# Two transformer layers on one core: operands split by ScalarE's rounding instead of a mask, a chunk's splitting moved behind the keys, first rows transposed tile by tile, epsilon put into the statistics

## Chip, cores, metric

The kernel runs on one core of a Trainium2 chip. The metric is the device time of one execution in microseconds. Engines are named as the profile does: PE (TensorE; PEld is its weight load), DVE (VectorE), ACT (ScalarE), POOL (GpSimd), SP (SyncE, whose queue issues most DMAs).

## What is computed

The reference, cut to what matters. `x` is [2, 512, 512] in float32; B=2, S=512, HID=512, INTER=1376.

```python
x = _layernorm(x + _L0_attn_ref(x, ...))   # retrieval from a memory M: q = elu(x@Wq.T+bq)+1 in
                                           # 8 heads, (q@M)/(q@z+1e-6), repeated, @ Wo.T
x = _layernorm(x + _L0_ffn_ref(x, ...))    # ternary weights, silu(gate)*up, truncated to int8 twice
x = _layernorm(x + _L1_attn_ref(x, ...))   # one head of 128: softmax(q@k.T/sqrt(128)) @ v, @ Wo + bo
x = _layernorm(x + _L1_ffn_ref(x, ...))    # silu(x@w_gate.T) * (x@w_up.T), @ w_down.T, all float32
```

with `_layernorm(x) = (x - mean) / sqrt(var + 1e-5)` over the last axis.

## The kernel before, in words

**Tiles.** A batch row block is 512 tokens: four tiles `x_b_t` of 128 tokens by 512 columns. Products want the columns on partitions, so the tiles are transposed on PE, 128x128 at a time, into a PSUM bank `pt`, and copied to SBUF. PSUM is one pool of eight banks of 128x512 (`psum`), handed out in turn: a new tile waits until the one eight before it is read.

**Order.** On PE, DVE, ACT and SP the order of instructions on each engine is set when the kernel is built, by the framework's scheduler; `tc.issue_after(i)` is a tie that puts what follows it behind instruction `i` in that order. POOL's order is the order of the program.[...]

**Layer 0, attention.** `load_x(0)` (L85) sends four tiles, on SP's and ACT's queues in turn; then come `wq_0`, `bq`, `z` and the other heads' weights on SP's queue (L307 to L311). `rise` (L108) is a set of products of `ones` with itself that no result uses. `transposed(xs[0], "a00", cuts=2)` (L444) transposes two tiles, then the other two, each time with four copies by ACT and DVE (L129). `queries` (L341) makes a head's queries, head 0 in two halves of 256 tokens. The heads' outputs, normalised, go on to layer 0's FFN (products L556 and L611), whose ternary values are checked and coded.

**Layer 1, attention.** For each batch: transposes, queries and keys (`pqk`, L842; evicted by ACT with bias, L847), values (`pv`, L855; DVE adds bv, L859). POOL adds `bo` to the rows (L906). Then scores (`psc`, L870), DVE's row maxima (L876), ACT's exponentials (L892), transposes of the probabilities (`pt_p`, L124), products with the values (`pot`, L927, copied to `ot`, L931), and `output` (L942: `po`, L944). `attended` (L947) divides by the sum and adds the row; `norm_a1` normalises: statistics on DVE, `root` (L160) and two `off` steps on POOL (L938, L939), and the scaling on ACT (L940).

**Layer 1, FFN.** Full float32 accuracy from three products in fp32r[...]: each operand is split into h, its upper part, l, the rest, and d, a combination of both. `cut` (L748) makes the upper part m on DVE by masking the lower bits away. `weight_parts` (L757) takes m, 4096·w by ACT (`big`, two buffers), h as ACT's copy of m, l = big − 4096·m and d = l − m on DVE. `row_parts` (L767) does so for rows. INTER is cut into eleven chunks, ten of 128 and one of 96; `turn = [6..10, 0..5]` is their order. The splitting of the first three chunks (`split_up(0)`, `(1)`, `(2)`; L790) lies within layer 1's attention: two while batch 1's transposes are copied, the third behind the last row maximum and ahead of the reciprocals. Later ones, and those of the down weights (`split_down`, L1096) and of the products' results (`split_tile`, L1103), are called in the loop over steps (L1163). `split_rows` (L970) transposes a batch's normalised rows and splits them; for batch 1 and for k > 0 ACT copies the bank to SBUF first (L982).

`up1` (L1071) is a step: gate and up products of one chunk and one batch (24 products, L1039), summed by ACT and DVE (`sum_up`), Silu on ACT and the product of both on DVE. The first step of a batch goes through its products block by block as rows become ready. `down1` (L1119) makes the down products (L1130) for one tile of 128 tokens, adds them, normalises and sends the rows; the very last tile is done in two halves of 256 columns (`cuts` = 2). Its `else` branch (L1145) is the end of the kernel: variance plus epsilon on DVE (L1147), power −1/2 on POOL (L1148), mean subtracted and the first half scaled on DVE (L1149, L1150), the other half on ACT (L1151), and two sends (L1155).

Of the kernel before, what the change touches and what calls it, by code (L numbers as in the profile page):

```python
# [19 lines left out]
P = 128  # L20
# [16 lines left out]
def kernel(  # L37
# [47 lines left out]
    def load_x(b):  # L85
        for t in range(NT):
            x = xp.tile([P, HID], F32, tag="x", name=f"x_{b}_{t}")
            eng = nc.scalar if b == 0 and t % 2 else nc.sync
            eng.dma_start(x, x_in[b, ts(t, P), :])
            xs[b].append(x)  # L90

    load_x(0)
    bq = const.tile([D, NH], F32, tag="bq", name="bq")
    z = const.tile([D, NH], F32, tag="z", name="z")

    make_identity(nc, ident)
# [8 lines left out]
    nc.vector.memset(ones, 1.0)  # L105
# [9 lines left out]
    def transposed(rows, name, cuts=0, in_turn=False):  # L115


        xt = xtp.tile([P, NK, S], F32, tag="xt", name=f"xt_{name}")
        pts = {}

        def turn(k, t, i=0):
            if (k, i) not in pts:
                pts[k, i] = psum(f"pt_{name}_{k}_{i}")
            return nc.tensor.transpose(  # L124
                pts[k, i][:, ts(t, P)], rows[t][:, ts(k, P)], ident
            )

        def copy(k, at, i=0):
            move = nc.vector.tensor_copy if k == 1 or k % 2 > in_turn else nc.scalar.copy  # L129
            copies.append(move(xt[:, k, at], pts[k, i][:, at]))  # L130

        if cuts:
            for i in range(cuts):
                for t in range(i * NT // cuts, (i + 1) * NT // cuts):
                    for k in range(NK):
                        turn(k, t, i)
                for k in range(NK):
                    copy(k, ts(i, S // cuts), i)
        else:
            done = None  # L140
            for k in range(NK):
                with ExitStack() as tied:
                    if in_turn and k:
                        tied.enter_context(tc.issue_after(done.ins))
                    for t in range(NT):
                        done = turn(k, t)
                copy(k, slice(0, S))
        return xt
# [152 lines left out]
    with tc.tile_pool(name="a0w", bufs=1) as a0w, tc.tile_pool(name="a0", bufs=2) as a0:  # L301
        wq = []
        for h in range(NH):
# [5 lines left out]
            if h == 0:  # L309
                nc.sync.dma_start(bq, bq_in)  # L310
                nc.sync.dma_start(z, z_in)  # L311
# [29 lines left out]
        def queries(b, xt, h, cuts=1):  # L341

            pq = psum(f"pq_{b}_{h}")
            for i in range(cuts):
                at = ts(i, S // cuts)
                for k in range(NK):
                    nc.tensor.matmul(  # L347
                        pq[:, at], wq[h][:, k, :], xt[:, k, at],
                        start=(k == 0), stop=(k == NK - 1),
                    )  # L350
# [7 lines left out]
            qs[b].append(q)  # L358

# [84 lines left out]
        xt = transposed(xs[0], "a00", cuts=2)  # L444
        for h in range(NH):
            queries(0, xt, h, 1 if h else 2)
# [296 lines left out]

    BIG = 4096.0
    MAIN, CROSS = 1.0 + 1.0 / BIG, 1.0 / BIG
    cutp = ctx.enter_context(tc.tile_pool(name="cutp", bufs=2))

    def cut(src, w, name):  # L748

        m = cutp.tile([P, 512], F32, tag="cut", name=f"m_{name}")  # L750
        p = src.shape[0]
        nc.vector.tensor_single_scalar(
            m[:p, :w].bitcast(I32), src.bitcast(I32), TOP12, ALU.bitwise_and
        )
        return m[:p, :w]

    def weight_parts(w, parts, name):  # L757

        h, l, d = parts
        m = cut(w, 512, name)  # L760
        big = cutp.tile([P, 512], F32, tag="big", name=f"big_{name}")
        nc.scalar.activation(big, w, AF.Copy, scale=BIG)
        nc.scalar.copy(h, m)
        nc.vector.scalar_tensor_tensor(l, m, -BIG, big, ALU.mult, ALU.add)
        return nc.vector.tensor_sub(d, l.bitcast(F32), m)  # L765

    def row_parts(src, m, parts):  # L767

        h, l, d = parts
        moved = nc.scalar.copy(h, m)  # L770
        nc.vector.tensor_sub(l, src, m)
        return moved, nc.vector.scalar_tensor_tensor(
            d, l.bitcast(F32), -BIG, m, ALU.mult, ALU.add
        )
# [15 lines left out]
    def split_up(j, room):  # L790
# [3 lines left out]
        for a in range(2):  # L794
# [5 lines left out]
            if n == P or a == 0:  # L800
                done = weight_parts(w, up_parts[j, a], f"gu{j}_{a}")
                continue

            u, m, w = (
                v.rearrange("p (k i) -> p k i", k=NK)
                for v in (up_parts[j, a][0], cut(w, NK * P // 2, f"gu{j}_{a}"), w)
            )
            nc.scalar.copy(u[:, :, : P // 2], m)
            done = nc.vector.tensor_sub(u[:, :, P // 2 :], w, m)
# [51 lines left out]

    probs = []
# [47 lines left out]
    table(AF.Silu, exponentials(1, got1, {1: copies[-4], 2: copies[-2]}))  # L910
    with tc.issue_after(scaled_max.ins):
        done = split_up(2, room1[6:] + take(4))
# [21 lines left out]
    def scalar_norm(x, stats, name):  # L934
# [3 lines left out]
        nc.gpsimd.tensor_tensor(off, mv[:, 0:1], rstd, ALU.mult)  # L938
        nc.gpsimd.tensor_scalar(off, off, -1.0, None, ALU.mult)  # L939
# [30 lines left out]
    def split_rows(b, room):  # L970

        parts, moved = [], []
        for k in range(NK):
            pt = psum(f"pt_f1{b}_{k}")
            for t in range(NT):
# [271 lines left out]
```

## Time and profile before

| quantity | value |
| --- | --- |
| median of 3 runs | 472.85 us (472.67 to 473.71) |
| profiled execution, its own time | 473.93 us |
| its span | 472.1 us |
| granted clock of PE, mean | 0.999 |
| products and transposes of PE | 1883 |
| instructions of DVE / ACT / POOL | 687 / 514 / 152 |
| last product ends | about 466.5 us in the span |

The profile is of one execution. Its time is a little above its span, which runs from the first to the last instruction recorded. A line of the timeline has the start, the length (of a run of equal instructions, all together), the engine and source line, the operation, `result<-operands`, shapes, `xcount`, and in brackets how long the engine had been idle and what released it. A line of the waits has the waiting engine, name and line, then what it waited for, then the total, the number of times and the longest. In the table of stages each engine has its busy time and the number of its instructions. PE's ends are modelled, so distances between starts say more than gaps.

### The profile page before, as it was taken

To read this page: it belongs to the slowest core of one execution; us is meant where nothing else is said; L and a number is where in the kernel's file an instruction comes from. 1 tells how busy PE (TensorE), PEld (TensorE's weight loads), DVE (VectorE), ACT (ScalarE), POOL (GpSimd) and SP (SyncE) were. 2 spreads that over 40 slices of the span, in tenths; PEclk is the share of its full clock that TensorE was granted. 3 is DMA by queue.
4 is the path that set the end of the run, shared out by engine and by line. 5 is a ranking of instruction groups with operands and counts; after the bars stand their busy time and mean duration, and the time that the engine had idled before them with its cause. 6 is when DMAs were issued, how large, how long until landed. Compare 5 with 4: busy or idle time off the path is not lost.

```text
span 472.1 us, 5813 instructions
## 1 busy us (share of the span) xinstructions
PE 464.4 (98%) x1883; PEld 330.7 (70%) x1883; DVE 348.9 (74%) x687; ACT 273.9 (58%) x514; POOL 116.7 (25%) x152
## 2 busy tenths in 40 slices
PE   9999999999999999999999999999999999999995
PEld 8454444434478788888866567888888888888885
DVE  1255677767857677755989989998975778999862
ACT  2343799557556876546755844675873575434221
POOL 0334101566460190400358031100000000023221
PEclk9999999999999999999999999999999999999999
DMA  8999800000015000213291000000000000000111
GB/s 313 381 328 347 339 1 1 0 0 1 2 57 185 3 1 1 92 47 80 72 369 68 1 0 2 0 2 0 1 0 0 1 1 1 0 24 22 45 46 45
DMA packets 15189, 33.99 MB, mean 72 GB/s; under 512 B 3440, under 2 KB 4336, under 8 KB 15152
## 3 DMA queue, kind: packets, MB, share of 16 engines
q1 hardware_dynamic: 14720, 32.85, 19.4%
q10 hardware_dynamic: 432, 0.66, 0.4%
q8 instruction: 22, 0.36, 0.3%
q14 instruction: 15, 0.12, 0.1%
HBM read 31.40 MB, written 2.10 MB: 71 GB/s over the span
## 4 chain that ended last, share of the span: by engine, by line
PE 66%; DVE 9%; ACT 8%; issue 4%; POOL 1%; POOLq 0%; DVEq 0%; ACTq 0%
PE pm L1039 17%; PE pg_f L556 9%; PE pu_f L556 8%; PE pc L1039 8%; PE pdm L1130 7%; PE pd_f L611 4%; PE pdc L1130 4%; DVE x L414 4%; PE po L392 2%; ACT y L405 2%; ACT t L424 2%; PE po L944 2%; PE pqk L842 1%; DVE mx L876 1%; DVE it_early L765 1%
## 5 line engine op out<-in xcount | busy, mean ns | idle before, releaser
L392 PE MATMUL po<-mw,q 128*128 128x512 f32 x128 | 57.2, 598 | 0.3 <-DVE mv_a L157 0.2
L347 PE MATMUL pq<-xt_a,wq 128*128 128x512 f32 (+1 forms) x136 | 56.4, 567 | 0.0
L163 POOL TENSOR_TENSOR rstd_f<-mv_f,ln_eps 128x1 f32<-128x1 f32 x15 | 4.3, 289 | 169.5 <-DVE mv_f L1141 127.6
L392 PEld LDWEIGHTS po<-mw,q 128*128 128x128 f32 x128 | 23.0, 189 | 32.2 <-issue 17.7
L347 PEld LDWEIGHTS pq<-xt_a,wq 128*128 128x128 f32 x136 | 25.5, 190 | 27.5 <-issue 25.7
L1039 PE MATMUL pm<-r,it_early 128*128 128x512 f32 x144 | 37.4, 390 | 0.4 <-ACT r L770 0.4
L1039 PE MATMUL pm<-r,ugu 128*128 128x512 f32 x152 | 37.7, 389 | 0.0
L1039 PEld LDWEIGHTS pm<-r,ugu 128*128 128x128 f32 x152 | 28.5, 188 | 5.9
L1039 PEld LDWEIGHTS pm<-r,it_early 128*128 128x128 f32 x144 | 27.0, 188 | 6.2 <-ACT r L770 0.7
L414 DVE SCALAR_TENSOR_TENSOR x<-po,den,x 128x511 f32<-128x511 f32 x40 | 29.8, 745 | 1.9
L185 ACT ACTIVATE ta_f<-y_f,below_half 128x512 int8<-128x512 f32 (+1 forms) x22 | 15.9, 723 | 23.7 <-DVE y_f L175 23.3
L409 POOL TENSOR_TENSOR y<-y,y 128x511 f32<-128x511 f32 x16 | 20.4, 1272 | 31.5 <-ACT y L405 30.8
L1049 DVE SCALAR_TENSOR_TENSOR ev_q<-pm,ev_q 128x512 f32<-128x512 f32 x27 | 18.4, 684 | 12.3 <-PE pm L1039 12.3
L582 DVE SCALAR_TENSOR_TENSOR it_f<-tb_f,ta_f 128x512 fp32r<-128x512 int16 (+1 forms) x22 | 15.2, 689 | 16.3 <-ACT tb_f L186 16.3
L353 ACT ACTIVATE e<-pq,bq 128x512 f32<-128x512 f32 x16 | 11.1, 692 | 25.8 <-PE pq L347 25.8
L556 PE MATMUL pg_f<-xh,tu 128*128 128x512 f32 x88 | 24.8, 401 | 0.0
L426 POOL TENSOR_SCALAR td<-wd,inv_down 128x512 fp32r<-128x512 f32 x11 | 18.6, 1708 | 22.0 <-DVE inv_down L219 22.0
L556 PE MATMUL pg_f<-xl,tu 128*128 128x512 f32 x88 | 23.6, 390 | 0.0
L556 PE MATMUL pu_f<-xh,tu 128*128 128x512 f32 x88 | 23.6, 389 | 0.0
L556 PE MATMUL pu_f<-xl,tu 128*128 128x512 f32 x88 | 23.5, 389 | 0.0
L1048 ACT ACTIVATE ev_q<-pc 128x512 f32<-128x512 f32 x27 | 15.9, 592 | 10.7 <-PE pc L1039 10.6
L396 ACT ACTIVATE den<-po,den_eps 128x1 f32<-128x1 f32 x64 | 14.5, 275 | 12.2 <-PE po L392 12.2
(302 smaller groups left out, 1115.0 us busy)
## 6 DMA issues: line engine op xcount, KB each, us to landing
gu<-in_gu SPq DMA_DIRECT2D x20, 512.0 KB, 7.8
wo<-in_wo SPq DMA_DIRECT2D x16, 512.0 KB, 7.3
wd<-in_wd SPq DMA_DIRECT2D x20, 256.0 KB, 5.1
wq<-in_wq SPq DMA_DIRECT2D x8, 256.0 KB, 4.0
out<-x SPq DMA_DIRECT2D x7, 256.0 KB, 2.0
x<-in_x SPq DMA_DIRECT2D x6, 256.0 KB, 5.8
wqkv<-in_wqkv SPq DMA_DIRECT2D x1, 768.0 KB, 10.8
x<-in_x ACTq DMA_DIRECT2D x2, 256.0 KB, 3.9
```

The lines of the kernel that those rows point to most:

```text
L185: nc.scalar.activation(a[:n], y, AF.Relu, bias=below_half[:n])
L347: nc.tensor.matmul(pq[:, at], wq[h][:, k, :], xt[:, k, at], start=(k == 0), stop=(k == NK - 1),)
L392: nc.tensor.matmul(po, qs[b][h0 + j][:, ts(t, P)], mw[:, h0 + j, :], start=True, stop=True,)
L409: nc.gpsimd.tensor_add(ys[0][:, :LAST], ys[0][:, :LAST], y[:, :LAST])
L414: steps.append(nc.vector.scalar_tensor_tensor(x[:, :LAST], four[j][:, :LAST], d, x[:, :LAST], ALU.mult, ALU.add))
L426: eng.tensor_scalar(out, w, factor, None, ALU.mult)
L556: nc.tensor.matmul(pp[a], t[:, a, i % NK, :], x2[b][i], start=(i == 0), stop=(i == 2 * NK - 1),)
L611: nc.tensor.matmul(pd, inter[b][c][:, ts(t, P)], td[c].bitcast(F32R), start=(c == 0), stop=(c == last),)
L1039: nc.tensor.matmul(p, w, x, start=(left[id(p)] == begun[id(p)]), stop=(left[id(p)] == 1))
L1048: nc.scalar.activation(ev, pc, AF.Copy, scale=CROSS)
L1049: nc.vector.scalar_tensor_tensor(ev, pm, MAIN, ev, ALU.mult, ALU.add)
L1130: nc.tensor.matmul(p[:, :w], got[j // 4][1][kind][:, j % 4], down_parts[j][kind][:, cols], start=(j == 0 and kind == kinds[0]), stop=(j == ...
```

## The change

What it does, part by part:

1. **Front.** `ones` is set first on DVE. The sends are x_0_0 (SP), x_0_1 (ACT), wq_0, x_0_2, x_0_3, wq_1, bq, z and the rest (SP). The first batch's tiles are transposed one by one, each into one bank (`first_rows`); ACT copies its first half and DVE its second. Head 0's products for a tile's 128 tokens follow behind the next tile's transposes, and head 1 behind all of them.
2. **Splitting.** The mask is gone. h is ACT's rounding of w·(1 − 2⁻¹³) into fp32r, read straight from the source, PSUM included (`upper`); l and d are made on DVE from h. The rows' copies from PSUM to SBUF are gone as well.
3. **Third chunk.** Its four ACT operations (h and `big` for gate and up) are tied behind the second batch's last key activation; its DVE operations stay behind the last row maximum.
4. **`off`** is one POOL instruction with two operations instead of two instructions.
5. **Start of the second FFN.** For batch 0, `split_rows` makes all sixteen transposes first, then the product `output(1, 3)`, and `attended(1, 3)` behind k = 0's DVE operations. The first step's products alternate between gate and up.
6. **Steps.** What a step splits is tied behind the Silu of the step before.
7. **End.** HID·epsilon is added to the first half's sum of squared deviations, once it is known, and the epsilon instruction at the end is gone; DVE scales and SP sends 320 columns, ACT 192.

```diff
-    load_x(0)
+    load_x(0, range(2))
...
+    nc.vector.memset(ones, 1.0)
     make_identity(nc, ident)
...
-    nc.vector.memset(ones, 1.0)
...
             if h == 0:
+                load_x(0, range(2, NT))
+            elif h == 1:
                 nc.sync.dma_start(bq, bq_in)
                 nc.sync.dma_start(z, z_in)
...
+        def first_rows(xt, t):
+
+            pt = psum(f"pt_a00_{t}")
+            for k in range(NK):
+                done = nc.tensor.transpose(pt[:, ts(k, P)], xs[0][t][:, ts(k, P)], ident)
+            pt = pt.rearrange("p (k t) -> p k t", k=NK)
+            nc.scalar.copy(xt[:, :2, ts(t, P)], pt[:, :2])
+            nc.vector.tensor_copy(xt[:, 2:, ts(t, P)], pt[:, 2:])
+            return done
+
+        def first_queries(pq, xt):
+
+            done = first_rows(xt, 0)
+            for t in range(NT):
+                if t + 1 < NT:
+                    with tc.issue_after(done.ins):
+                        done = first_rows(xt, t + 1)
+                with tc.issue_after(done.ins):
+                    done = query_products(pq, xt, 0, ts(t, P))
+            return done
...
+    UPPER = 1.0 - 2.0**-13
...
+    def upper(h, src):
+        return nc.scalar.activation(h, src, AF.Copy, scale=UPPER)
+
+    def weight_upper(w, h, name):
+
+        upper(h, w)
         big = cutp.tile([P, 512], F32, tag="big", name=f"big_{name}")
         nc.scalar.activation(big, w, AF.Copy, scale=BIG)
-        nc.scalar.copy(h, m)
-        nc.vector.scalar_tensor_tensor(l, m, -BIG, big, ALU.mult, ALU.add)
-        return nc.vector.tensor_sub(d, l.bitcast(F32), m)
+        return big
+
+    def weight_parts(w, parts, name, big=None):
 
         h, l, d = parts
-        moved = nc.scalar.copy(h, m)
-        nc.vector.tensor_sub(l, src, m)
-        return moved, nc.vector.scalar_tensor_tensor(
-            d, l.bitcast(F32), -BIG, m, ALU.mult, ALU.add
+        if big is None:
+            big = weight_upper(w, h, name)
+        nc.vector.scalar_tensor_tensor(l, h.bitcast(F32), -BIG, big, ALU.mult, ALU.add)
+        return nc.vector.tensor_sub(d, l.bitcast(F32), h.bitcast(F32))
+
+    def row_parts(src, parts):
+
+        h, l, d = parts
+        upper(h, src)
+        nc.vector.tensor_sub(l, src, h.bitcast(F32))
+        return nc.vector.scalar_tensor_tensor(
+            d, l.bitcast(F32), -BIG, h.bitcast(F32), ALU.mult, ALU.add
         )
...
+    room2 = room1[6:] + take(4)
+    with tc.issue_after(moved.ins):
+        bigs2 = [
+            weight_upper(
+                gus[turn[2]][:, a].rearrange("p k i -> p (k i)"), room2[3 * a], f"gu2_{a}"
+            )
+            for a in range(2)
+        ]
...
-        done = split_up(2, room1[6:] + take(4))
+        done = split_up(2, room2, bigs2)
...
-        nc.gpsimd.tensor_tensor(off, mv[:, 0:1], rstd, ALU.mult)
-        nc.gpsimd.tensor_scalar(off, off, -1.0, None, ALU.mult)
+        nc.gpsimd.tensor_scalar(off, mv[:, 0:1], rstd, -1.0, ALU.mult, ALU.mult)
...
+        if behind:
+            for k in range(NK):
+                turn(k)
+            with tc.issue_after(pts[-1][1].ins):
+                p = behind[0]()
         for k in range(NK):
...
+            if not behind:
+                turn(k)
             parts.append(room[3 * k : 3 * k + 3])
...
+            done = row_parts(pts[k][0], parts[k])
+            if behind and k == 0:
+                with tc.issue_after(done.ins):
+                    behind[1](p)
         return parts, done
...
         if j == 0:
-            run([p + q for p, q in zip(passes0, passes1)], True)
+            run([[x for y in zip(p, q) for x in y] for p, q in zip(passes0, passes1)], True)
...
             nc.vector.bn_stats(st[:, i, :], x[:, cols])
+            if i == 0 and cuts > 1:
+
+                m2 = st[:, 0, 2:3]
+                nc.vector.tensor_scalar(m2, m2, HID * LN_EPS, None, ALU.add)
...
-            nc.vector.tensor_scalar(rstd, mv[:, 1:2], LN_EPS, None, ALU.add)
-            nc.gpsimd.tensor_tensor(rstd, rstd, minus_half, ALU.pow)
+            nc.gpsimd.tensor_tensor(rstd, mv[:, 1:2], minus_half, ALU.pow)
             nc.vector.tensor_scalar(x, x, mv[:, 0:1], None, ALU.subtract)
+            w = 320
             nc.vector.tensor_scalar(x[:, :w], x[:, :w], rstd, None, ALU.mult)
             nc.scalar.activation(x[:, w:], x[:, w:], AF.Copy, scale=rstd)
...
-        up1(b, j)
+        before, moved = moved, up1(b, j)
...
+        with tc.issue_after(before.ins):
+            if ahead <= last and b == 1:
+                split_up(
+                    ahead, room0 if ahead in (3, 6) else take(6 if turn[ahead] < last else 4)
+                )
+                ahead += 1
```

## The prediction, made before the changed kernel was run

> **What bounds the kernel now.** I read the page first, then PE's waits, then the stages, then the timeline around each place where PE pauses.
>
> ```profile
> PE 464.4 (98%) x1883; PEld 330.7 (70%) x1883; DVE 348.9 (74%) x687; ACT 273.9 (58%) x514; POOL 116.7 (25%) x152
> PE 66%; DVE 9%; ACT 8%; issue 4%; POOL 1%; POOLq 0%; DVEq 0%; ACTq 0%
> ```
>
> PE is busy for 98% of the span and is most of the chain that ended last. So only what lies around PE can change: the time ahead of its first matmul, the pauses between, and what follows its last. All of PE's pauses put down to another engine:
>
> ```profile
> PE rise L110 <- DVE ones L105: 1.2, 1, 1.2
> PE pm L1039 <- ACT r L770: 0.4, 1, 0.4
> PE po L392 <- DVE mv_a L157: 0.2, 1, 0.2
> PE po L944 <- ACT ot L931: 0.2, 1, 0.2
> ```
>
> Stages (columns: length, then busy time of PE, PEld, DVE, ACT, POOL):
>
> ```profile
> 273.10:285.85 12.75, 12.34 (x49) 7.81 (x49) 11.12 (x21) 5.36 (x9) 4.63 (x16) 1.00 0.00 1
> 285.85:292.00 6.15, 6.08 (x25) 4.71 (x26) 6.05 (x13) 2.68 (x5) 0.00 (x0) 1.00 0.01 1
> 309.90:405.80 95.90, 95.90 (x424) 79.39 (x423) 78.18 (x139) 61.38 (x110) 1.04 (x2) 1.00 0.00 1
> 466.50:472.10 5.60, 0.05 (x1) 0.00 (x0) 1.96 (x6) 0.51 (x1) 0.73 (x1) 0.95 0.14 47
> ```
>
> The third line matters most: in the long stretch of the second FFN's products PE has no gap, while DVE has 17.7 us of slack and ACT 34.5. Work taken from DVE there buys nothing directly. Gaps are at 273, at 285 and in the 5.6 us after the last product. A wait's figure can understate a pause, since ends are modelled. So I also took the distance between PE's starts: a full-width product of this FFN starts 0.227 after the one before it.
>
> [...] `rise` and the first transposes start 0.213 apart until 7.1 to 7.4 us, then 0.109.[...] L764 and L765 start 1.68 apart while POOL adds bo (L906, to 257.5) and 0.60 apart after.[...]
>
> **1. The front.** `ones` moves to the head of DVE's memsets, four of which stand 0.03 apart before it: PE's first matmul at 1.0 instead of 1.155, −0.15. From there to 11.21, where head 1's products begin, PE is gap-free. So transposing tile by tile removes no pause; it only reorders. Head 0 changes from 16 products at 0.216 to 32 of 128 columns; the same width runs at 0.112 each (values, L855): 32×0.112 − 16×0.216 = +0.13. On data: two x tiles and the first weights are 768 KB, and the trace has 700 KB landed at 4.0 and 1060 at 5.0, so x_0_0, x_0_1 and wq_0 are there by about 4.4, as early as needed; x_0_2 follows wq_0 on SP's queue and is wanted at about 6.3, x_0_3 at 7, with 1280 KB landed at 5.7. ACT's copy ends about 6.1 and DVE's 6.6, first products at 6.3 (half of them in slow clock). Queued past by the moved loads: wq_1 is third behind them, wanted at 11. Sum −0.02; bounds −0.3 (the clock is released a bit earlier in relation to the work) and +0.3 (a copy is late, or the release falls later).
>
> **2. Third chunk, ACT's part behind the keys.**
>
> ```profile
> 271.45 0.60 ACT L763 CAST it_early<-m_gu 128x512 fp32r<-128x512 f32 x1
> 271.96 0.61 ACT L763 CAST ugu<-m_gu 128x512 fp32r<-128x512 f32 x1
> 272.48 0.57 ACT L931 COPY ot<-pot 128x512 f32<-128x512 f32 x1
> 273.10 3.70 PE L944 MATMUL po<-wo,ot 128*128 128x512 f32 x8 [0.20 <-ACT ot L931]
> ```
>
> ACT's in-order stream has two casts of the third chunk ahead of the `ot` copy that PE wants next. PE's transposes start at 270.99, 16×0.109, so they end at 272.74; the product starts at 273.10, and one interval later on is 0.10 too long: pause 0.46. With both casts gone, the copy follows the table warm-up (271.54) and its pot, and ends at 272.1. Pause gone: −0.46. What it displaces: four ACT operations of 0.62 go to just behind the second qk activation. Before, that activation is at 260.46, held by casts that waited for DVE's masks; without them only the two `big` buffers hold ACT, each until one DVE operation of 1.68 has read it, and my estimate is 257. So the four end at 260.1, and the first exponential starts at 262.69 before. DVE loses six masks there (0.48 each) but starts its two-input operations earlier, under POOL's adds: eight of them from 250.1, about five at 1.68 and three at 0.6, end at 260.3 instead of 260.99. If all eight went at 1.68 it would be 263.5 and scores would be late by 2.5; POOL's adds end at 257.5, which excludes it. Bounds −0.46 and 0.
>
> **3. `off` in one.** POOL's chain for a normalised tile is 1.40 from start to start (0.27+0.65+0.28+0.20); one operation less, 1.12. Tile 3 before: off ready 282.73, ACT 282.77 to 283.58, transposes 283.52. After: all of it 0.46 earlier by step 2 and 0.4 by this, ready near 282.3, with PE wanting it at 282.5. No gain of its own, it is what lets step 4 begin; slack 0.2.
>
> **4. Start of the second FFN.**
>
> ```profile
> 284.46 0.68 DVE L752 TENSOR_SCALAR m_x<-pt_f 128x512 int32<-128x512 int32 x1
> 285.18 0.62 ACT L770 CAST r<-m_x 128x512 fp32r<-128x512 f32 x1
> 285.84 0.30 PEld L1039 LDWEIGHTS pm<-r,it_early 128*128 128x128 f32 x2 [0.65 <-ACT r L770]
> 285.85 0.73 PE L1039 MATMUL pm<-r,it_early 128*128 128x512 f32 x2 [0.41 <-ACT r L770]
> 286.64 0.19 PEld L1039 LDWEIGHTS pc<-r,it_early 128*128 128x128 f32 x1 [0.50 <-DVE r L772]
> ```
>
> Mask, then cast, then product: 0.68+0.62 behind the first transposed tile. In PE's starts the excess over 0.227 is 0.58 at 285.85 and 0.12, 0.23, 0.11 after: 1.03. After the change ACT rounds straight out of PSUM (one step of 0.62), and PE has the transposes of k=1..3 (12×0.109=1.3) and two products of `output` (0.86) between the first part's source and its use: 2.2 of cover for 0.62. Gate and up alternate, so the first d is the fifth product, not the third; a k stays 6 products, 1.36, against two DVE operations of 0.67. PE without a pause (285.85 − 0.46 − 0.58) starts at 284.81, so d0 is wanted at +4×0.227 = 285.72, d1 at +10×0.227 = 287.08, d3 at +22×0.227 = 289.80. DVE: d0 done 284.9, attended(1,3) 0.75, l1 and d1 1.3: 286.95; four more of 0.67: 289.65. These two slacks are only 0.13 and 0.15; d0's is 0.8. −1.03; bounds −1.15 and −0.4.
>
> **5. Splitting.** 65 masks leave DVE (22×0.48, 11×0.42, 24×0.45 and the rows': about 28 us) and seven copies leave ACT (0.58 each). All lie beside a gap-free PE: 0. The new ties put a step's splitting behind the preceding Silu on ACT; behind it there wait the next step's evictions. At the down products PE waits 0.19 for uwd (L765, 409.14). A mask of 0.42 leaves the chain ahead of that part, so it is ready about 0.2 before PE: −0.15; bounds −0.19 and +0.4.
>
> **6. The tail.**
>
> ```profile
> 467.51 0.21 DVE L1141 BATCH_NORM_AGGREGATE mv_f<-st 128x2 f32<-128x12 f32 x1
> 467.75 0.15 DVE L1147 TENSOR_SCALAR rstd_f<-mv_f 128x1 f32<-128x1 f32 x1
> 467.99 0.73 POOL L1148 TENSOR_TENSOR rstd_f<-rstd_f,minus_half 128x1 f32<-128x1 f32 x1 [5.97 <-DVE rstd_f L1147]
> 468.76 0.51 ACT L1151 ACTIVATE x<-x,rstd_f 128x256 f32<-128x256 f32 x1 [5.89 <-POOL rstd_f L1148]
> 469.30 0.35 ACTq L1155 DMA_DIRECT2D out<-x  x1
> ```
>
> The epsilon is added while the second half's products run, so 0.15 and its hand-over leave the path: power at about 467.80, −0.18. With 192 columns ACT takes about 0.45, not 0.51; DVE's 320 about 0.43, not 0.35, but DVE's send was 0.16 ahead. −0.05 more. The halves land 1.7 and 1.9 after issue; other sizes, same order. −0.22; bounds −0.35 and −0.05.
>
> **Sum.** −0.02 −0.46 −1.03 −0.15 −0.22 = −1.88. Against it I set +0.15 for one of the three slacks of 0.13 to 0.2 not holding: −1.73. The profiled execution took 473.93 (span 472.1, the rest outside it): it gives 472.20. The median of runs is 472.85, 1.08 below it; 472.85−1.73 = 471.1. A difference of 0.2%, 0.95 us, is about what a measurement of this kernel can tell from no change.
>
> **Rivals.** (A) The pauses form again in the same places: transposes wait for the normalised tile 3, d1 and d3 come late, and the front does nothing because PE was full there. Speaks for it: slacks of 0.1 to 0.2 worked out from one execution. Against: each step removes work from the very chain. −0.46, half of step 4 and half of the tail would be left of the gain, less 0.4 lost anew: −0.46−0.5−0.1+0.4 = −0.66, 472.2. (B) Slower: ACT's queue in the second FFN. A batch-1 step with a split_up and two split_downs has four roundings and scalings (4×0.62), two evictions and a Silu (1.8) and 4×0.62: 6.8 against 5.44 of PE (24×0.227). Bound to wait behind the Silu, they hold the next evictions, and PE runs out of banks: 1.35 for each such step, three of them 4.0, less 1.73: 475.1. It decides once an eviction comes more than one step late. Against: ACT has 34 us of slack there, and the step after has only 1.8 of ACT work, 8.6 in 10.9 us. (C) The change doesn't do what it says: interleaving has no effect as PE waits for the first part anyway: within A.
>
> **How the numbers follow.** My forecast, 0.71 (470.2 to 471.9); A 0.20; B 0.09. Low end: front −0.3, start −1.15, tail −0.35, down −0.19, −0.46 are −2.45 all together, 470.4, and half a span of runs (0.3) below: 470.1. High end: A with as much above: 472.6. Faster by over 0.2% (below 471.9): 0.70 and 0.04 of A, 0.74; same: 0.17; slower: B, 0.09.
>
> **What would show it.** No PE wait at `po` L944 and at the first pm; the first pm near 284.7; POOL's power 1.2 after the last product instead of 1.5; DVE busy near 321, PE still near 464. I'm wrong if PE shows a pause in the products or scores, or if head 1 begins after 11.3.

## The result and the profile after

| | before | changed |
| --- | --- | --- |
| median, first nine executions of each | 473.53 us | 471.99 us (471.51 to 472.99) |
| ratio, 95% interval | | 0.9976 (0.9966 to 0.9987) |
| profiled execution, its span | 473.93, 472.1 | 471.99, 470.0 |
| mean of all executions in this study | 473.31 (149) | 472.14 (25) |

The ratio stands for −1.1 us (−1.6 to −0.6), the long means for −1.17. Forecast were −1.73. The time lies in the range, the sign was right, and the gain is about two thirds of the forecast. Measured from the 472.85 that the prediction started from, a median of three, it is 0.86, half of the forecast. The spans of the two profiles differ by 2.2 (before rounding), more than the medians; that is part of the puzzle.

Busy times and the chain of the changed kernel's page:

```profile
PE 463.0 (99%) x1899; PEld 330.7 (70%) x1899; DVE 327.9 (70%) x622; ACT 268.1 (57%) x507; POOL 114.4 (24%) x141
PE 72%; ACT 7%; DVE 5%; issue 3%; POOL 0%; POOLq 0%; DVEq 0%; ACTq 0%
```

All waits of PE:

```profile
PE rise L110 <- DVE below_half L105: 1.0, 1, 1.0
PE po L401 <- DVE mv_a L137: 0.2, 1, 0.2
```

Of the four waits of before, the two in layer 1 (po, L944, and the first pm, L1039) are gone. Stages (length, then busy time of PE, PEld, DVE, ACT, POOL):

```profile
272.23:283.90 11.67, 11.67 (x50) 7.62 (x49) 10.19 (x21) 5.17 (x9) 3.95 (x12) 1.00 0.01 1
283.90:290.00 6.10, 6.10 (x27) 4.86 (x26) 6.03 (x10) 0.74 (x3) 0.00 (x0) 1.00 0.00 1
307.87:403.73 95.86, 95.86 (x424) 79.39 (x423) 69.29 (x112) 61.43 (x114) 1.04 (x2) 1.00 0.00 1
464.13:470.00 5.87, 0.28 (x3) 0.08 (x1) 1.93 (x5) 0.46 (x1) 0.84 (x1) 0.71 0.13 45
```

PE has no gap from the po products on. In the long stretch DVE lost 27 instructions and 8.9 us of work (78.18 to 69.29), and the stretch is as long as before: 95.86 against 95.90. Nothing was to be had there, as the prediction said. Now the `ot` copy, on the timeline:

```profile
270.45 0.20 ACT L836 ACTIVATE warm_Silu<-ln_eps 1x1 f32<-1x1 f32 x1
270.49 1.91 PE L125 MATMUL pt_p<-ident,prob 128*128 128x128 f32 x16
270.74 0.59 ACT L953 COPY ot<-pot 128x512 f32<-128x512 f32 x1
272.23 3.60 PE L965 MATMUL po<-wo,ot 128*128 128x512 f32 x8
```

No cast stands between the table's first Silu and the copy; it ends 0.9 before PE wants it, and the products follow the sixteen transposes (270.49 + 16×0.109 = 272.23) without a gap. The start of the second FFN:

```profile
282.33 2.07 ACT L763 ACTIVATE r<-pt_f 128x512 fp32r<-128x512 f32 x4 [0.44 <-PE pt_f L1002]
282.96 0.69 DVE L784 TENSOR_TENSOR r<-pt_f,r 128x512 fp32r<-128x512 f32 x1 [0.24 <-ACT r L763]
283.69 0.69 DVE L785 SCALAR_TENSOR_TENSOR r<-r 128x512 fp32r<-128x512 f32 x1
283.90 1.49 PE L1071 MATMUL pm<-r,it_early 128*128 128x512 f32 x4
```

ACT rounds the first block at 282.33, 1.6 before its use. (PE's record of 283.90 is an early one, 0.03 behind the start of `output` at 283.87; the next start is 284.53, two products of 0.43 and 0.23 after 283.87. There is no gap.) And the end:

```profile
465.37 0.21 DVE L1174 BATCH_NORM_AGGREGATE mv_f<-st 128x2 f32<-128x12 f32 x1
465.62 0.49 DVE L1181 TENSOR_SCALAR x<-x,mv_f 128x512 f32<-128x512 f32 x1
465.67 0.84 POOL L1180 TENSOR_TENSOR rstd_f<-mv_f,minus_half 128x1 f32<-128x1 f32 x1 [6.02 <-DVE mv_f L1174]
466.54 0.46 ACT L1184 ACTIVATE x<-x,rstd_f 128x192 f32<-128x192 f32 x1 [6.05 <-POOL rstd_f L1180]
467.03 0.36 ACTq L1186 DMA_DIRECT2D out<-x  x1
```

The epsilon's instruction is gone, but the power, 0.73 long before, takes 0.84. From PE's last start to the end of the span it was 5.87; it is 5.82. Two more lines of the kernel before will matter: DVE's subtraction at the end, between the epsilon and the power, and an earlier power of the same size:

```profile
467.82 0.48 DVE L1149 TENSOR_SCALAR x<-x,mv_f 128x512 f32<-128x512 f32 x1
276.89 0.55 POOL L164 TENSOR_TENSOR rstd_a<-rstd_a,minus_half 128x1 f32<-128x1 f32 x1
```

Where the time went, from the starts of PE in both profiles (distance between two marks, before and changed):

| from, to | before | changed | difference | forecast |
| --- | --- | --- | --- | --- |
| span's start, head 1 | 11.21 | 10.70 | −0.51 | −0.02 |
| head 1, first po of layer 1 | 261.89 | 261.53 | −0.36 | step 2: −0.46 with the 0.10 behind po |
| first po, first down product | 132.94 | 131.75 | −1.19 | step 4: −1.03, and that 0.10 |
| first down product, last product | 60.23 | 60.15 | −0.08 | step 5: −0.15 |
| last product, end | 5.87 | 5.82 | −0.05 | step 6: −0.22 |

The sum is −2.19. Two rows don't fit: the front gave 0.5 where nothing was forecast, and the tail next to nothing. And if all this is so, why are the times only 1.1 apart?

### The profile page after: what moved, and what is told of

Its sections match the earlier page's. It is cut to its first block, busy times and chain, and to the rows that moved or that the text cites. A ratio compares the mean times of both kernels' runs of the same rounds, so it can differ in the third digit from the quotient of the medians.

```text
span 470.0 us, 5725 instructions
## 1 busy us (share of the span) xinstructions
PE 463.0 (99%) x1899; PEld 330.7 (70%) x1899; DVE 327.9 (70%) x622; ACT 268.1 (57%) x507; POOL 114.4 (24%) x141
## 4 chain that ended last, share of the span: by engine, by line
PE 72%; ACT 7%; DVE 5%; issue 3%; POOL 0%; POOLq 0%; DVEq 0%; ACTq 0%
PE pm L1071 17%; PE pg_f L567 9%; PE pu_f L567 8%; PE pc L1071 8%; PE pdm L1159 7%; PE pd_f L622 4%; PE pdc L1159 4%; DVE x L423 4%; PE pqk L853 3%; PE po L401 2%; ACT y L414 2%; ACT t L433 2%; PE pv L866 2%; PE pot L949 1%; PE po L965 1%
## 5 line engine op out<-in xcount | busy, mean ns | idle before, releaser
L961 ACT ACTIVATE x<-x,off_f,rstd_f 128x512 f32<-128x512 f32 x7 | 5.7, 816 | 27.7 <-POOL off_f L960 27.7
```

## The experiments

Theories. P (phase): PE's clock is released, that is, its starts go from 0.213 to 0.11 apart (the trace's record of a granted clock of 1.00 begins at 7.33 in before and at 5.78 in changed), at a moment that differs between executions, and the 0.5 of the front is that. F (front): the new order gained it. L (lock): at the end POOL's power is held up by DVE's subtraction, 0.48 or 0.49 long, beside which it took 0.73 and 0.84. Ahead of each result stands what was expected, on record before the run. Times are means of the executions, with their number; "changed" is 472.14, "before" 473.31. The kernel before was timed beside each of the five groups of runs and had means of 473.24 to 473.40, so means of different groups are compared as they stand. "Error" is one standard error. "Release" is the moment in us from the span's start, "head 1" the start of its first product, "tail" the time from PE's last start to the end of the span.

**e1, the changed kernel again.** No edit.

> The changed kernel once more, unaltered. In the two profiles so far head 1's first product starts at 11.21 (before) and 10.70 (after), and PE's starts close up from 0.213 to 0.11 apart at about 7.4 and 5.75. Theory P (phase): the moment at which PE's clock is released differs from execution to execution, each us of it moves head 1 by 0.5 us, and the front itself gives about +0.1 to +0.3. Then head 1 starts here at about 7.7 + 0.5 x release (10.2 to 11.5, wherever the release falls), and everything after head 1 keeps its distances to within 0.1. Theory F (front): the tile-by-tile order itself gained the 0.5, and head 1 starts at 10.7 again whatever the release. Time about 472.0 to 472.4.

Measured: 472.11 (16), ratio 0.9975 (0.9966 to 0.9984). Release at about 6.8, head 1 at 11.01: 7.60 + 0.5×release. The same kernel started head 1 0.31 later than in its first profile. P holds, F falls. The release is read from PE's starts: 0.213 apart ahead of it, 0.11 after. Over all sixteen profiles with one of the two fronts as they are (sorted by front and release; the last columns are used further down):

| profile | release | head 1 | head 1 − release/2 | start of maximum − head 1 | pause at head 8 |
| --- | --- | --- | --- | --- | --- |
| before, old front | 7.3 | 11.21 | 7.54 | 24.98 | 0 |
| e13, old | 6.4 | 10.74 | 7.55 | 24.92 | 0 |
| e14, old | 5.7 | 10.39 | 7.56 | tied | 0 |
| e12, old | 5.3 | 10.22 | 7.57 | 26.56 | 1.08 |
| e16, old | 5.2 | 10.19 | 7.57 | tied | 0 |
| e2, old | 4.9 | 10.03 | 7.56 | 25.73 | 0.25 |
| e4, new front | 7.2 | 11.18 | 7.59 | 23.83 | 0 |
| e5, new | 7.1 | 11.16 | 7.59 | 24.38 | 0 |
| e1, new | 6.8 | 11.01 | 7.60 | 25.65 | 0.17 |
| e6, new | 6.5 | 10.87 | 7.63 | 26.72 | 1.24 |
| e7, new | 5.9 | 10.70 | 7.75 | 26.49 | 1.00 |
| changed, new | 5.8 | 10.70 | 7.81 | 24.05 | 0 |
| e9, new | 5.4 | 10.62 | 7.93 | 24.08 | 0 |
| e10, new | 4.7 | 10.26 | 7.93 | tied | 0 |
| e15, new | 4.1 | 9.98 | 7.95 | tied | 0 |
| e3, new | 3.9 | 9.91 | 7.95 | 25.69 | 0.20 |

With the old front head 1 is at 7.55 + release/2 in all six profiles, to within 0.02, over releases from 4.9 to 7.3. Transposes start 0.213 apart until the release and 0.109 after it: work takes about twice its time until then, hence the half. What sets the moment is not shown; in these sixteen profiles it fell anywhere from 3.9 to 7.3. So in the first pair of profiles (7.3 and 5.8) the release alone accounts for −0.78, and the new front for +0.27, which leaves the −0.51.

**e2 and e12, the old front in the changed kernel**, twice the same.

```diff
-    load_x(0, range(2))
+    load_x(0)
...
-        with tc.issue_after(queries(0, xt, 0).ins):
-            queries(0, xt, 1)
+        xt = transposed(xs[0], "a00", cuts=2)
```

> The changed kernel with part 1 undone: loads, memsets, first transposes and head 0 as before. Theory P: head 1 at 7.52 + 0.5 x release (its value in the profile of before), so with the phase averaged out the time is that of the changed kernel less 0.1 to 0.3. Theory F: head 1 at 11.2, time 0.5 above the changed kernel. The prediction on record had the front at -0.02 (bounds -0.3 and +0.3).

> The kernel of e2 once more, unaltered. In e2 the power at the end took 0.55 beside DVE's subtraction, in four profiles with the new front 0.84, though DVE and POOL began equally far apart in all. If it is chance of the execution, this one may show 0.84; if it belongs to this build, 0.55 again. Time: the changed kernel less 0.1 to 0.5.

Measured: 471.44 (6) and 471.88 (6), together 471.66 with a standard error of 0.18; ratios 0.9966 and 0.9968. That is 0.5 below the changed kernel, with an error of 0.2. Head 1 at 7.56 and 7.57 + 0.5×release. In e12 the power at the end took 0.84, in e2 0.55, in the same program, so it differs between executions of one build. From e2:

```profile
465.12 0.51 DVE L1170 TENSOR_SCALAR x<-x,mv_f 128x512 f32<-128x512 f32 x1
465.17 0.55 POOL L1169 TENSOR_TENSOR rstd_f<-mv_f,minus_half 128x1 f32<-128x1 f32 x1 [6.02 <-DVE mv_f L1163]
```

**e5, the new front alone** in the kernel before (the front's part of the diff, nothing else).

> The kernel before with part 1 alone. From the runs so far: head 1 starts at 7.54 to 7.56 + 0.5 x release with the old front (two profiles), and at 7.59, 7.60, 7.81, 7.95 + 0.5 x release with the new one (releases 7.2, 6.8, 5.8, 3.9). Theory P: this kernel is slower than before by 0.05 to 0.4, about 0.2, the more the earlier the release; head 1 falls on that line. Theory F: 0.5 faster than before. The prediction on record: -0.02.

Measured: 473.28 (13), ratio 1.0 (0.9991 to 1.0008): no change, as the prediction had it (−0.02). The table tells more: measured by head 1 − release/2, the new front loses 0.03 to 0.05 with a late release and 0.4 with an early one, since PE, its starts 0.11 apart, runs into ACT's copies. From e3, release 3.9:

```profile
4.93 0.81 ACT L337 COPY xt_a<-pt_a 128x256 f32<-128x256 f32 x2 [2.48 <-PE pt_a L335]
5.33 0.86 DVE L338 COPY xt_a<-pt_a 128x256 f32<-128x256 f32 x2 [4.31 <-ACT xt_a L337]
5.35 0.98 PEld L325 LDWEIGHTS pq<-xt_a,wq 128*128 128x128 f32 x8 [0.26 <-ACT xt_a L337]
```

ACT copies a bank's first half, and DVE's copy of the other half follows (the view has it wait for ACT's, idle for 4.31 before); PE's load waits 0.26 for ACT's.

**e3, a narrower subtraction in the tail.**

```diff
-            nc.vector.tensor_scalar(x, x, mv[:, 0:1], None, ALU.subtract)
             w = 320
-            nc.vector.tensor_scalar(x[:, :w], x[:, :w], rstd, None, ALU.mult)
+            nc.vector.tensor_scalar(x[:, w:], x[:, w:], mv[:, 0:1], None, ALU.subtract)
+            nc.vector.tensor_scalar(
+                x[:, :w], x[:, :w], mv[:, 0:1], rstd, ALU.subtract, ALU.mult
+            )
```

> The changed kernel, but at the end DVE subtracts the mean from ACT's 192 columns only, and does the other 320 in one operation after POOL's power. Theory L (lock): in both profiles the power ends 0.41 after DVE's 512-wide subtraction ends (468.72 after 468.30 before, 466.51 after 466.11)[...]; with 192 columns the subtraction ends about 0.25 earlier, so the power takes about 0.6 from its issue instead of 0.84, and the output is sent 0.25 earlier. Rival: the power's length is its own (0.73, 0.84) and nothing moves; loss of up to 0.05 if the combined DVE operation is longer.

```profile
465.04 0.32 DVE L1182 TENSOR_SCALAR x<-x,mv_f 128x192 f32<-128x192 f32 x1
465.09 0.68 POOL L1180 TENSOR_TENSOR rstd_f<-mv_f,minus_half 128x1 f32<-128x1 f32 x1 [6.02 <-DVE mv_f L1174]
466.27 0.33 SPq L1188 DMA_DIRECT2D out<-x  x1
```

The power ends at 465.77, 0.41 after the subtraction's end at 465.36, as in before (468.72 after 468.30) and changed (466.51 after 466.11). Two widths, 512 and 192 columns, and one distance: L holds. The size was over-expected, as 192 columns take 0.32 and not 0.25: the power is 0.16 shorter, the tail from PE's last start 5.76 instead of 5.82. The mean, 472.10 (18), can't show so little.

**e7, the epsilon instruction back in the tail.**

```diff
-            nc.gpsimd.tensor_tensor(rstd, mv[:, 1:2], minus_half, ALU.pow)
+            nc.vector.tensor_scalar(rstd, mv[:, 1:2], LN_EPS, None, ALU.add)
+            nc.gpsimd.tensor_tensor(rstd, rstd, minus_half, ALU.pow)
```

> The changed kernel with the epsilon instruction back in the tail (320/192 kept). Prediction's step 6: the power starts 0.18 later and all behind it too, tail from the last product +0.18. Theory L: DVE's 512-wide subtraction starts only 0.06 to 0.1 later, and the power ends 0.41 after the subtraction in either case, so +0.06 to +0.1; in a run[...] (0.55 in one of the runs so far) +0.18.

Measured: tail 5.88 against 5.82 to 5.83, so +0.06, as L had it and not 0.18. Time 472.07 (20), which can't show so little. The power again ended 0.40 after the subtraction: the epsilon did not set the power's end.

**e4, the old order at the start of the second FFN** (rounding from PSUM kept).

```diff
-    x3[0], done = split_rows(
-        0, rooms[0], (lambda: output(1, t), lambda p: attended(1, t, p))
-    )
+    x3[0], done = split_rows(0, rooms[0])
...
-            run([[x for y in zip(p, q) for x in y] for p, q in zip(passes0, passes1)], True)
+            run([p + q for p, q in zip(passes0, passes1)], True)
```

> The changed kernel with part 5 undone: output(1,3) and attended(1,3) ahead of the transposes, gate and up of the first step block by block and not alternating; ACT still rounds straight from PSUM. Prediction's step 4: ACT's part alone takes the mask's 0.68 off the first wait (0.58 left nothing) but the second and third waits (0.12+0.23+0.11) stay or grow, since d is wanted third: 0.3 to 1.0 of the 1.03 comes back. Rival: the rounding from PSUM alone removes the wait, and no more than 0.2 comes back.

```profile
284.65 1.08 PE L1068 MATMUL pm<-r,it_early 128*128 128x512 f32 x3
285.00 0.30 PEld L1068 LDWEIGHTS pm<-r,it_early 128*128 128x128 f32 x2 [0.18 <-DVE r L784]
285.73 0.19 PEld L1068 LDWEIGHTS pc<-r,it_early 128*128 128x128 f32 x1 [0.43 <-DVE r L785]
```

PE waits for l (L784) and then d (L785), 0.12+0.11+0.16+0.11 in starts; first po to first down product 132.16 against 131.75. Of the 1.19 in the table 0.10 belongs to `po`, so the start of the FFN gained 1.09. 0.41 of it belongs to the order; the other 0.68 came with the rounding, as much as the mask, the first link of the chain, had taken. (The new order with the mask still in place was not run.) Time 472.41 (17), +0.27 with an error of 0.14.

**e6, the third chunk's ACT steps called where they were**, and **e9**, the same with a tie behind the last exponential.

```diff
-    with tc.issue_after(moved.ins):
-        bigs2 = [
...
-        done = split_up(2, room2, bigs2)
+        done = split_up(2, room2)
```

> The changed kernel with part 3 undone: the third chunk's ACT steps back behind the last row maximum, still by rounding. Prediction's step 2: the ot copy is again behind ACT's operations of the third chunk, now four of 0.62 where casts stood, so PE pauses ahead of po: 0.46 or more (two of the four could run before the table load), and everything behind stays at its distance. Rival: without the masks these operations start early enough and PE's pause is under 0.1, so the gain came from the rounding and not from the move.

```profile
PE pt_a L125 <- DVE x L149: 5.3, 3, 2.0
PE pq L325 <- DVE xt_a L127: 1.0, 1, 1.0
234.77 0.63 ACT L763 ACTIVATE it_early<-gu 128x512 fp32r<-128x512 f32 x1 [6.20 <-PE pd_f L622]
```

Measured: 481.05 (4), 9 above changed. A miss for both readings: the steps did not land where the casts were. The tie of `split_up(2)` is to a DVE instruction and orders DVE; before, it was the mask on DVE that kept ACT's casts back. With the mask gone nothing did, and the first rounding went into ACT's stream at 234.77, where ACT stood idle 6.20 for its room, with layer 0's outputs behind it: PE waits 5.3 for rows. That is not all of the 9. PE was busy for only 0.86 of the 3.5 us from 235.0 to 238.5, and the granted clock was at half, 0.51 on average, from 238.5 to 245.4 (thirteen transposes from 241.65 on start 0.217 apart). That the one brought the other is not shown. PE was busy for 4.23 there, so about 2.1 were lost to the clock (half of it, an estimate). The mean granted clock was 0.991 or 0.992 in all four executions of e6, 0.996 or more in those of the changed kernel. With the 1.24 of another wait, at head 8 (see below), 5.3 + 2.1 + 1.24 are 8.6 of the 8.96 that head 1 to the first `po` is longer. So part 3's tie is not a refinement; rounding needs it. In e9 the block stands in front of `ot`:

```diff
     table(AF.Silu, moved)
+    with tc.issue_after(moved.ins):
+        bigs2 = [
```

> Part 3 undone again, now with a tie: the third chunk's four ACT steps stand behind the last exponential and the table load, ahead of the ot copy, as the two casts did before. Reckoned from the profile of the changed kernel: last exponential and its sum end at 269.15, table and first Silu to 270.65, four steps of 0.62 to 273.1, ot copy to 273.7, and PE wants ot at 272.23: PE pauses 1.5 ahead of po (0.47 before, with two casts), and DVE's four steps behind them come later than PE's next needs, which may add up to 1. Rival: something else had held ot, and PE pauses no more than 0.5.

```profile
272.06 0.61 ACT L769 ACTIVATE big_gu<-gu 128x512 f32<-128x512 f32 x1
272.58 0.56 ACT L953 COPY ot<-pot 128x512 f32<-128x512 f32 x1
273.19 1.12 PE L965 MATMUL po<-wo,ot 128*128 128x512 f32 x2 [0.85 <-ACT ot L953]
```

PE's start is 1.02 late, another 0.10 follows, and 0.74+0.10 at the second half's `ot` (280.92), behind DVE's four steps: 1.96 in all, with 1.5 and up to 1 expected. Time 474.28 (11), 2.1 above changed. Where these steps stand on ACT decides 2 us.

**The missing half microsecond.** The rows of the difference table without the front make −1.68, and changed is 1.17 below before. In e12 PE has a wait that neither of the first two profiles has:

```profile
36.78 1.28 DVE L197 TENSOR_REDUCE mx_up<-gu 128x1 f32<-128x512 f32 x2 [1.04 <-DMA gu<-in_gu]
37.98 0.68 DVE L130 COPY xt_a<-pt_a 128x512 f32<-128x512 f32 x1
38.72 1.55 PE L347 MATMUL pq<-xt_a,wq 128*128 128x512 f32 x3 [0.82 <-DVE xt_a L130]
```

DVE's maximum of the first gate and up weights waits until they have landed, and DVE's copy of batch 1's transposes, which head 8 (batch 1's first) wants, is queued behind it. In the table above the pause is the excess of the maximum's start over head 1 + 25.59, and 0.10 an interval later: with 25.65 to 26.72 it is 0.17 to 1.24, with 25.0 or less nothing, in all thirteen profiles that have this order (e8 is the thirteenth: 24.80, no pause). The landing differs between executions (the maximum starts at 34.7 to 37.6), and a head 1 that starts early brings the pause nearer. The trace of before, read for the prediction, has the same order and DVE's wait in it, only without a pause of PE:

```profile
36.19 1.28 DVE L197 TENSOR_REDUCE mx_up<-gu 128x1 f32<-128x512 f32 x2 [1.95 <-DMA gu<-in_gu]
```

At 24.98 behind head 1 it had 0.6 to spare, while landings differ by 2.9.

**e10 and e15, the maximum behind the copies** in the changed kernel, twice the same.

```diff
-                mx_up = largest(
+                with tc.issue_after(copies[-1].ins):
+                    mx_up = largest(
```

> The changed kernel with one tie more, in a part that the change did not touch: DVE's maximum of the first gate and up weights is put behind its copies of batch 1's transposes. Reading of ten profiles: that maximum starts when gu lands (34.7 to 37.6), holds the copies behind it, and PE pauses at head 8 by the amount that this start exceeds head 1's start + 25.6 (0, 0, 0, 0, 0, 0.06, 0.10, 0.14, 0.90, 1.13). Expected: no PE pause between 36 and 42 in any profile; the mean time 0.2 to 0.4 below the changed kernel's. Rival: the pause only moves to the product that needs the scales, and nothing is won.

> e10 once more: the changed kernel with that tie. 471.6 in e10 with six executions; expected 471.5 to 471.7 again, that is the sum of the named places (-1.7) below 473.3.

```profile
38.05 0.68 DVE L127 COPY xt_a<-pt_a 128x512 f32<-128x512 f32 x1
38.65 1.26 DVE L177 TENSOR_REDUCE mx_up<-gu 128x1 f32<-128x512 f32 x2
```

Measured: 471.60 (6) and 471.54 (8), together 471.56; ratios 0.9964 and 0.9962. 0.58 below changed (error 0.14), with no pause at head 8 and none in its place. The spread of the executions falls as well, from a standard deviation of 0.54 to 0.30. The time is 1.74 below before, close to the forecast's sum; but before lacks the tie (see e14).

**e13 and e14, the kernel before again, and with the same tie.**

> The kernel before, unaltered. Head 1 at 7.55 + 0.5 x release, head 8 paused by max(0, start of the maximum - head 1 - 25.59). If the wait at head 8 belongs to all these kernels, it shows up in about half of the profiles here too; if it comes with the change, not. Time 473.3.

> The kernel before with the maximum of gu put behind the copies of batch 1's transposes, nothing else. If before suffers from the wait at head 8 as the changed kernel does (0.4 there), it becomes 0.3 to 0.5 faster, 472.9; if not, it stays at 473.3, and the changed kernel had lost 0.4 to 0.5 at a place that nobody touched.

Measured: 473.32 (14) and 473.12 (14), ratios 0.9997 and 0.9994 (0.9985 to 1.0003). The tie is worth about 0.2 in before (error 0.11) and 0.58 in the changed kernel; the difference, 0.39, has an error of 0.18. With the tie in both, the changed kernel is 1.56 (error 0.13) below before. The pause occurred in none of the three profiles of before and e5 with this order, and in six of the other ten; so few can differ by chance. Releases were late in those three, 6.4 to 7.3, and a late release moves head 1 back, away from the pause.

**e16, e15 with the old front.**

> e15 with the old front: tells the front's own effect where no wait at head 8 blurs it. From the profiles (7.55 against 7.59 to 7.95 + 0.5 x release): 0.05 to 0.4 faster than e15, about 0.2. From e5 (front alone, no change): the same as e15 within 0.15.

Measured: 471.53 (7) against 471.54. Without the wait at head 8 the front's two forms are alike, with an error of 0.15. The 0.5 of e2 and e12 does not return. In e16's profile the power at the end took 0.55, as in e2.

**e8 and e11, versions made from this.** The old front with `ones` first, six products of `rise` (e8) or seven (e11), and a tail in which DVE does nothing large during the power; e11 has the tie of e10 too.

```diff
-    for _ in range(8):
+    for _ in range(7):
...
-            nc.vector.tensor_scalar(x, x, mv[:, 0:1], None, ALU.subtract)
+            off = small.tile([P, 1], F32, tag="off", name="off_last")
+            nc.vector.tensor_scalar(off, mv[:, 0:1], -1.0, None, ALU.mult)
+            nc.scalar.activation(x[:, w:], x[:, w:], AF.Identity, bias=off)
+            nc.vector.tensor_scalar(
+                x[:, :w], x[:, :w], mv[:, 0:1], rstd, ALU.subtract, ALU.mult
+            )
```

> A version made from the findings: the changed kernel with the old front, but ones set first and six products of rise instead of eight (they only fill time: four records fewer are 0.44 at full clock), and a tail in which DVE subtracts nothing while POOL raises to the power: ACT subtracts the mean from its 192 columns, DVE does its 320 in one operation after the power. Theory P: head 1 at 7.06 + 0.5 x release, unless PE then waits for x tiles (x_0_0 landed at 3.4, x_0_1 at 3.7, x_0_2 and x_0_3 at 5.1), which would take back up to 0.3 where the release is early. Theory L: power 0.55 long, output sent 0.2 to 0.3 earlier after the last product than in the changed kernel. Together 0.6 to 0.9 below the changed kernel, about 471.3. Rival:[...] with less of rise in front nothing is won there.

> The version with old front, ones first and the new tail, now with seven products of rise (with six, PE waited 0.35 for the first x tile) and with the maximum behind the copies. Head 1 at 7.25 to 7.5 + 0.5 x release, no pause at head 8, power 0.55 long. About 1.0 below the changed kernel, 471.0; rival: as e8_best, 0.6 to 0.8 below.

```profile
464.82 0.55 POOL L1169 TENSOR_TENSOR rstd_f<-mv_f,minus_half 128x1 f32<-128x1 f32 x1 [6.03 <-DVE mv_f L1163]
464.84 0.15 DVE L1172 TENSOR_SCALAR off_last<-mv_f 128x1 f32<-128x1 f32 x1
465.03 0.46 ACT L1173 ACTIVATE x<-x,off_last 128x192 f32<-128x192 f32 x1 [5.39 <-DVE off_last L1172]
465.40 0.45 DVE L1174 TENSOR_SCALAR x<-x,mv_f,rstd_f 128x320 f32<-128x320 f32 x1 [0.41 <-POOL rstd_f L1169]
```

That is e8: the power is 0.55 long, the tail 5.59 (e11: 5.60) against 5.82. Times 471.26 (5) and 471.17 (5), ratios 0.9964 and 0.9953 (0.994 to 0.9967): e11 has the lowest mean, 2.1 below before, 1.0 below changed and 0.40 (error 0.18) below the changed kernel with the tie alone; e8 and e11 are not told apart. The shorter `rise` won nothing in these two profiles: releases of 4.8 and 4.2, head 1 at 7.53 and 8.04 + release/2, with PE waiting 0.35 for the first tile in e8 and for the third and for copies in e11. That part of the expectation failed; a late release, where it should pay, did not come up.

## Why the prediction was right or wrong

**The front (step 1)**: no change in time, as forecast (e5: ratio 1.0; e16 against e15: 0.01). The 0.5 (error 0.2) by which e2 and e12 were faster with the old front speaks against it; without the wait at head 8, in e16, it is not there. The parts of the sum were off: PE's first matmul came 0.11 earlier and not 0.15, and the tile-by-tile order cost up to 0.4 when the release was early. What it left out is that the release varies by over 3 us, half of which goes into the time: head 1 began anywhere from 9.91 to 11.21. It named this only as a bound of ±0.3. Its base was also too low: the three runs shown had a median of 472.85, the long mean is 473.31. The first pair of profiles alone would have misled: −0.51 at head 1, of which −0.78 is phase.

**Step 2**: right in place and size: −0.36 and the 0.10 behind `po`. DVE's two-input operations ended at 259.4, or 259.9 on the time of before, with 260.3 reckoned, so the reckoning of 1.68 and 0.6 each held: they start 1.49 to 1.78 apart while POOL adds `bo` (245.30 to 257.04), 0.60 after. What it did not see is that the move is a condition of the rounding (e6).

**Step 3**: right in its end: no pause ahead of the transposes. Tile 3 was scaled by 281.88, and PE's first transpose of it began at 282.02, a slack of 0.14 where 0.2 was reckoned. On the time of before (0.51 later) that is 282.39, so the scaling ended 1.19 earlier; the prediction's 0.46 and 0.4 add up to less.

**Step 4**: right. 1.09 where 1.03 was reckoned, and its slacks held. The split, 0.68 by the rounding and 0.41 by the order, came from e4.

**Step 5**: 0 in the long stretch, right. At the down products it was too large: −0.06 to −0.10 against −0.15. The wait of 0.19 that it read is that of PE's weight load; in PE's own starts the pause there was 0.04 (0.266 against 0.227).

**Step 6 failed.** "0.15 and its hand-over leave the path" was wrong: −0.05 instead of −0.22. The chain was not epsilon, then power. In both profiles POOL's power ended 0.41 or 0.42 after DVE's 512-wide subtraction, and that began only 0.06 earlier relative to PE's last product. The waits view did not show it, as the whole 0.73 counts as busy; the length of 0.73 against 0.55 for the same power elsewhere in the same trace (L164, at 276.89) did, before any run. The prediction had looked at such pairs only where DVE's operation has two tensor inputs (1.68 beside POOL's adds, 0.60 after); at the end DVE's has one (0.48), and it is POOL's power that takes longer. What decides whether the power is held is not shown: DVE's recorded start was 0.05 ahead in all ten profiles with the new tail and 512 columns, and the power took 0.84 in eight and 0.55 in e2 and e16 (where DVE's 512 columns took 0.51 instead of 0.48 or 0.49). Both of these have the old front. Whether the build shifts how often it is held, worth 0.3 in the tail (5.52 and 5.53 against 5.82), can't be told from three profiles with the old front.

**The sum failed in a term it did not have.** Added without the front the traces give −1.68 where the forecast had −1.71 with its reserve (−1.86 + 0.15). The executions gave −1.17. The forecast took the 262 us between head 1 and step 2 as fixed, without saying so and without a reason; the one trace at hand had no pause of PE near head 8, though it had DVE's wait of 1.95 there. The stretch is not fixed: at head 8 PE is paused by 0 to 1.2, depending on when gu lands. The tie that removes the pause takes 0.58 from the changed kernel and about 0.2 from before, and with it in both the gain is 1.56. Why it takes more from the changed kernel, by 0.39 with an error of 0.18, is not explained: with the old front (e2, e12) the order of instructions on every engine is the same as before until the second layer, and the wait was there. Whether it is chance, of the release above all, or something like the place of the data stays open.

**Rivals.** A gave 472.2, near the time measured. It was right that the front does nothing and that the tail gives less, but no pause formed again in the places it named at the transposes and the first products; the rest was lost at head 8. B did not occur: the long stretch is as long as before, with ACT at 61.43. The range held. The forecast gain was 0.6 too large: head 8 took 0.4 to 0.6 of it, the tail 0.17 and the down products 0.07, and the reserve of 0.15 stands on the other side.

## What to carry to other kernels

One trace without a gap does not make a stretch fixed: look for an engine's queue in which an operation that waits for a DMA stands ahead of one that PE wants (here DVE's maximum ahead of its copy, up to 1.24 at head 8), even where PE does not pause this time. Compare two traces by distances between marks, and take the clock's release at the start out first; here head 1 moved by up to 1.3 us with it. Take a pause of PE from the distance between its starts, not from the wait of its weight load (0.04 against 0.19 at the down products). A short operation that is longer than its like elsewhere in the same trace (0.73 against 0.55) may be held by something, even where the waits view shows nothing.

## What the hardware showed that was not expected

- PE's release, its starts going from 0.213 to 0.11 apart, fell anywhere from 3.9 to 7.3 us, and with the old front the first stage follows it closely (head 1 at 7.55 + half of it, to 0.02, in six profiles).
- A 128x512 tensor_scalar of DVE in SBUF with one tensor input took 0.49, 320 columns 0.39, 192 columns 0.32. Where the one of 512 or 192 columns stood beside POOL's 128x1 power and held it, the power ended 0.40 to 0.42 after it (before, changed, e3, e7).
- The same program showed that power at 0.55 and at 0.84 in two executions (e2, e12).
- In e6, where PE had been busy for 0.86 of 3.5 us, the granted clock fell to half for 6.8 us in the midst of the kernel and came back.
